# A two-layer perceiver on one core: small vector operations go to GpSimd, ScalarE and PSUM, and TensorE takes half the sums of the last recurrence

## The chip, the cores and the metric

The kernel runs on one core of one Trainium2 chip. Five engines of the core matter here. TensorE (PE in the profile; PEld is its weight load) multiplies matrices into PSUM, the accumulator memory of eight banks. VectorE (DVE) and ScalarE (ACT) read and write both SBUF and PSUM. GpSimd (POOL) works on SBUF here. SyncE (SP) issues most DMAs. Each engine takes its instructions in one fixed order, and an instruction that waits holds all that stand behind it on its engine.

The metric is the device time of one execution in microseconds (us), as the median of several runs. Lower is better.

## The reference, cut to what matters

The input `x` is 64 sequences of 32 tokens of 256 channels, that is 2048 tokens; `ctx` is 64 context sequences of 257 rows. Six layers follow each other, each added to `x`:

```python
x = x + cross_attention(layernorm(x), ctx, mask)        # stage 0 of the kernel
x = x + rwkv(layernorm(x))                              # stage 1
x = x + top2_experts(layernorm(x))                      # stage 2
x = x + quantized_cross_attention(layernorm(x), ctx)    # stage 3
x = x + state_space(layernorm(x))                       # stage 4
x = x + top1_experts(layernorm(x))                      # stage 5
```

Three details are touched by the change. Every layernorm (and the RMS norm inside the quantized attention) needs `1/sqrt(v + eps)`. The quantized attention rounds its rows to integers before a projection:

```python
scale = 127.0 / max(max(abs(x)), 1e-05)                 # per row
x_int = clip(round(x * scale), -128.0, 127.0)
```

The state-space layer keeps, for each of 512 channels, 16 states, and sums them with `C`:

```python
h = exp(A[None] * dt[:, :, None]) * h + dt * B_t * x_t
y = einsum('bdn,bn->bd', h, C_t) + D * x_t              # n = 16 states
```

The last layer computes all 8 experts (256 to 512 to 256 channels) with an exact gelu between.

## The kernel before, in words

The 2048 tokens are 4 blocks (`NBLK`) of 512 tokens (`BT`). Within a block, token-major tiles have 128 tokens (`P`) on the partitions. Stages 0, 1 and 2 work on blocks; stage 3 on 8 halves of 256 tokens, each of two tiles of 4 sequences, cut into 32 steps that `run` (L757) takes in order; stages 4 and 5 on blocks again. `layers` (L1280) writes the order by hand: the steps of stage 3 are laid between the blocks of stages 2 and 4 (`on(8, True)` and the like), and the recurrence of one block (`recur`) stands beside the attention or the experts of another. The program is then laid out as one fixed list per engine by a scheduler, which goes by the order of the text and its own costs; engines meet at semaphores.

**`_rsqrt`** (L76) makes `1/sqrt` without a table: `v = scale * in + eps` (L85), a first guess from the integer bits of `v` by a shift (L87) and a multiply-add (L88), all on VectorE, and then three Newton steps of four operations (L90 to L93) on the engine `eng`, which is GpSimd unless the caller gives VectorE. `_stats` (L107) calls it for each layernorm; stage 3 calls it for `dq` and `dy`.

**Stage 3.** `queries` (L712) prepares a half: mean and variance, `x - mean` into `xn` (L722), the rounding in `_quant_rows` (L341), and the step size `dq` (L728, L729). `_quant_rows` takes the row maximum, its scale and reciprocal, multiplies each tile by it and adds a constant that rounds (L350), and takes the constant off again into bfloat16 (L351). `finish` (L767) does the same for the attention's output `y`, which the trace calls `o` (L781 to L785). `attend` (L801) prepares one tile: `kl` (L828) is a PSUM result times a row of step sizes, `klm` (L830) spreads it with a mask. `back` (L923) divides by the softmax sums: `rs` is multiplied by a weight scale (L931), then by `pl` (L932), spread, and brought to `rt` through TensorE and a ScalarE copy (L946).

**Stage 4.** `recur` (L1078) loops over 16 states `n` and, in each, over two pairs of 128-channel groups (`c2` = 0 and 2). For one pair GpSimd multiplies `g` = dt x times B (L1096, 128x1024); ScalarE writes `h` = exp(A dt) into PSUM (L1100), twice; VectorE scans it (L1101) and multiplies by C into `hc` (L1102), twice; GpSimd adds `hc` to `y` (L1107; the trace calls `y` `xc`). After the loop GpSimd multiplies by the gate `zs` (L1110), and TensorE projects (L1122, or `end`, L1141, for the last block). `h` has two PSUM buffers (`psh`). For blocks 0 to 2 `_norm` (L1118) then makes the normalized residual `xe`.

**Stage 5.** `block` (L1236) loops over 8 experts times 4 groups of 128 hidden channels: two matrix products into `u` (L1251), an evacuation with bias by ScalarE (L1253), one gelu for each expert's 4 groups (L1255), and two products into `acc` with the expert before (L1259). `u` lies in the pool `psu` (one bank) or `ps` (two banks, tag `s`): for blocks 2 and 3 two of three go to `ps`. At the end of a block the result is transposed back through `rT` (L1272) and written out (L1273, L1275). The text puts the last recurrence (`recur(3)`) between the experts of block 1 and block 2; the scheduler lays the experts of block 2 beside it, and the experts of block 3 come last.

Of the kernel before, what the change touches and what calls it, by code (L numbers as in the profile page):

```python
# [75 lines left out]
def _rsqrt(k, out, parts, tag, pool=None, eng=None):  # L76


    nc, pool, f = k.nc, pool or k.small, out.shape[-1]
    eng = eng or nc.gpsimd  # L80
    n = out.shape[0]
    v, r, t = (pool.tile([P, f], F32, name=f"rs_{q}", tag=f"rs_{q}{tag}")[:n] for q in "vrt")
    at = 0
    for in_, scale, eps in parts:
        nc.vector.tensor_scalar(v[:, at : at + in_.shape[-1]], in_, scale, eps, ALU.mult, ALU.add)  # L85
        at += in_.shape[-1]
    nc.vector.tensor_scalar(r.bitcast(I32), v.bitcast(I32), 1, None, ALU.logical_shift_right)  # L87
    nc.vector.tensor_scalar(r.bitcast(I32), r.bitcast(I32), -1.0, 1597463007.0, ALU.mult, ALU.add)  # L88
    for step in range(3):
        eng.tensor_tensor(t, r, r, ALU.mult)  # L90
        eng.tensor_tensor(t, t, v, ALU.mult)
        eng.tensor_scalar(t, t, -0.5, 1.5, ALU.mult, ALU.add)
        eng.tensor_tensor(out if step == 2 else r, r, t, ALU.mult)  # L93
# [247 lines left out]
def _quant_rows(k, src, floor, ints, am):  # L341


    nc, n = k.nc, src.shape[1]
    nc.vector.tensor_reduce(am, src, AX.X, ALU.max, apply_absolute_value=True)
    sc = k.small.tile([P, n], F32, name="qsc", tag=f"q_sc{n}")
    nc.vector.tensor_scalar(sc, am, floor, 1.0 / 127.0, ALU.max, ALU.mult)
    nc.vector.reciprocal(sc, sc)
    for t in range(n):
        nc.vector.tensor_scalar(src[:, t, :], src[:, t, :], sc[:, t : t + 1], MAGIC, ALU.mult, ALU.add)  # L350
    nc.vector.tensor_scalar(ints, src, MAGIC, 127.0, ALU.subtract, ALU.min)  # L351
# [318 lines left out]
def _stage3(k, w, tmp):  # L670
# [41 lines left out]
    def queries(h):  # L712
        b, j0 = divmod(2 * h, 4)
        v = halves[h] = Ctx()
        v.xs = [k.x[b][:, j, :] for j in range(j0, j0 + 2)]

        mv = _moments(k, v.xs, "3")
        xn = k.wk3.tile([P, 2, D], F32, name="xn3", tag="xn3")  # L720
        for f in range(2):
            nc.vector.tensor_scalar(xn[:, f, :], v.xs[f], mv[:, f, 0:1], None, ALU.subtract)  # L722
        v.xq = k.wk3.tile([P, 2, D], BF16, name="xq", tag="xq")
        am = k.small.tile([P, 2], F32, name="am", tag="q_am")
        _quant_rows(k, xn, 3.1622776e-11, v.xq, am)
        dq = v.dq = k.small.tile([P, 2], F32, name="dq", tag="dq")
        _rsqrt(k, dq, [(mv[:, :, 1], 1.0 + RMS_EPS, RMS_EPS * LN_EPS)], "3")
        nc.vector.tensor_tensor(dq, dq, am, ALU.mult)  # L728
        nc.vector.tensor_scalar(dq, dq, 1e-5, qsc, ALU.max, ALU.mult)  # L729
# [37 lines left out]
    def finish(xs, o4):  # L767
# [13 lines left out]
        _quant_rows(k, y, 1e-8, yq, am)  # L781
        dy = k.small.tile([P, 2], F32, name="dy", tag="dy")
        _rsqrt(k, dy, [(ss, 1.0 / D, RMS_EPS)], "3y")
        nc.vector.tensor_tensor(dy, dy, am, ALU.mult)
        nc.vector.tensor_scalar(dy, dy, 1e-5, osc, ALU.max, ALU.mult)  # L785
# [15 lines left out]
    def attend(g, j, xq, dq, o4):  # L801
# [25 lines left out]
        kl = k.small.tile([P, 4], F32, name="kl", tag="kl3")  # L827
        nc.vector.tensor_tensor(kl, last_ps[:, P : P + 4], kb[:, :, 2 * P], ALU.mult)  # L828
# [94 lines left out]
        def back():  # L923
# [7 lines left out]
            nc.vector.tensor_scalar(rs, rs, mw[:, 2:3], None, ALU.mult)  # L931
# [14 lines left out]
            nc.scalar.copy(rt.rearrange("p w g i l -> p w l g i"), rt_ps.rearrange("p w (l g i) -> p w l g i", l=2, g=2))  # L946
# [25 lines left out]
def _stage4(k, w, wk):  # L972
# [44 lines left out]
    def ahead(b):  # L1017
# [3 lines left out]
        v.mv, v.rstd = _stats(k, xs, "4")  # L1021
        x2 = [tmp([P, 2, D], "xn4") for _ in range(2)]
# [55 lines left out]
    def recur(b, v, mem=None):  # L1078
# [4 lines left out]
        own, more = (mem, 1) if mem else (wk, 0)  # L1083
        dtx = wk.tile([P, C, BT], F32, name="dtx", tag="dtx", bufs=1)
# [6 lines left out]
        for n in range(N):  # L1091
            bc = own.tile([P, 2, BT], F32, name="bc", tag="bc", bufs=2 + more)
            nc.sync.dma_start(bc, bc_rows[n].partition_broadcast(P))
            for c2 in range(0, C, 2):
                g = own.tile([P, 2, BT], F32, name="g", tag="g", bufs=2 + more)
                nc.gpsimd.tensor_tensor(g, dtx[:, c2 : c2 + 2], bc[:, 0:1, :].to_broadcast([P, 2, BT]), ALU.mult)  # L1096
                hc = own.tile([P, 2, BT], F32, name="hc", tag="hc", bufs=2 + more)
                for c in range(2):
                    h = ph([P, BT], "h")
                    nc.scalar.activation(h, dt, AF.Exp, scale=A[:, c2 + c, n : n + 1])  # L1100
                    nc.vector.tensor_tensor_scan(h, h, g[:, c, :], 0.0, ALU.mult, ALU.add)  # L1101
                    nc.vector.tensor_tensor(hc[:, c, :], h, bc[:, 1, :], ALU.mult)  # L1102
                if n == 0:
# [4 lines left out]

        for c2 in range(0, C, 2):
            nc.gpsimd.tensor_tensor(y[:, c2 : c2 + 2], y[:, c2 : c2 + 2], v.zs[:, c2 : c2 + 2], ALU.mult)  # L1110
# [6 lines left out]
        for j in range(4):  # L1117
            _norm(k, xn[j], xs[j], v.mv, v.rstd, j)  # L1118
# [43 lines left out]
def _stage5(k, w, out):  # L1162
# [12 lines left out]
    def ps(shape, name, free=False):  # L1175

        return k.ps.tile(shape, F32, name=name, tag="s") if free else k.psu.tile(shape, F32, name=name, tag="u")
# [58 lines left out]
    def block(b, v):  # L1236
# [3 lines left out]
        for n in range(E * H + H):  # L1240
            e, q = divmod(n, H)
            if e < E:
# [6 lines left out]
                u = ps([P, BT], "up", b >= 2 and n % 3 > 0)  # L1249
# [3 lines left out]
                nc.scalar.activation(hid[e][:, q, :], u, AF.Identity, bias=b1)  # L1253
                if q == H - 1:
                    nc.scalar.activation(hid[e], hid[e], AF.Gelu)  # L1255
# [10 lines left out]
        for j2 in range(0, 4, 2):  # L1266
            rT = ps([P, 2, D], "rT", b >= 1)
# [178 lines left out]
```

## Time and profile before

| | us |
|---|---|
| time, median of 3 runs | 2037.06 (2034.74 to 2038.57) |
| the profiled execution's own time | 2031.43 |
| its span, first to last instruction | 2029.6 |
| busy: PE / DVE / POOL / ACT | 1604.5 / 1372.5 / 1062.8 / 986.5 |
| GpSimd waiting for VectorE's first guess (L90 on L88) | 178.6, 41 times |
| first recurrence, beside attention and experts of stage 2 | 767 to 1015 |
| second recurrence, beside attention and experts of stage 5 | 1115 to 1345 |
| third recurrence, the same | 1420 to 1690 |
| last recurrence, beside the experts of block 2 | about 1716 to 1887 |
| the experts of block 3, alone | 1910 to the end |

How to read it. A stretch such as 767 to 1015 is in us from the first instruction. A row of the stretch view gives, for one stretch, its length and then the busy time of PE, PEld, DVE, ACT and POOL, each with its number of instructions in brackets, the granted TensorE clock as a share of full speed, the DMA share and GB/s. A row of a group gives line, engine, operation, output<-inputs, shapes and count, and behind the bar the busy time in us, the mean ns of one, and the engine's idle time just before it with what ended it. A row of one line's view gives the shortest, median and longest duration in ns.

### The profile page before, as it was taken

To read this page: it belongs to the slowest core of one execution; us is meant where nothing else is said; L and a number is where in the kernel's file an instruction comes from. 1 tells how busy PE (TensorE), PEld (TensorE's weight loads), DVE (VectorE), ACT (ScalarE), POOL (GpSimd) and SP (SyncE) were. 2 spreads that over 40 slices of the span, in tenths; PEclk is the share of its full clock that TensorE was granted. 3 is DMA by queue.
4 is the path that set the end of the run, shared out by engine and by line. 5 is a ranking of instruction groups with operands and counts; after the bars stand their busy time and mean duration, and the time that the engine had idled before them with its cause. 6 is when DMAs were issued, how large, how long until landed. Compare 5 with 4: busy or idle time off the path is not lost. (4 is left out here: it accounts for less than half of the span.)

```text
span 2029.6 us, 20217 instructions
## 1 busy us (share of the span) xinstructions
PE 1604.5 (79%) x6323; PEld 820.7 (40%) x6323; DVE 1372.5 (68%) x2475; ACT 986.5 (49%) x2144; POOL 1062.8 (52%) x1189
## 2 busy tenths in 40 slices
PE   4775957759989888766788878878879777788698
PEld 3333524425645543433344434443434324333443
DVE  4588587576475458989965877864777786687400
ACT  3454443313455254444427746736647545576232
POOL 5344656413133215776650776871576766899200
PEclk9677877868989988556689778989779888899799
DMA  6764324210000201121101212401122212333021
GB/s 226 231 187 145 115 73 146 64 42 22 21 21 1 63 28 42 53 63 52 53 26 54 73 53 83 114 21 48 63 50 77 82 53 54 104 118 104 31 83 42
DMA packets 88379, 151.26 MB, mean 75 GB/s; under 512 B 7740, under 2 KB 52300, under 8 KB 86224
## 3 DMA queue, kind: packets, MB, share of 16 engines
q1 hardware_dynamic: 85428, 148.75, 24.0%
q10 hardware_dynamic: 2844, 1.22, 0.2%
q8 instruction: 50, 0.82, 0.2%
q14 instruction: 57, 0.47, 0.1%
HBM read 139.03 MB, written 10.92 MB: 74 GB/s over the span
## 5 line engine op out<-in xcount | busy, mean ns | idle before, releaser
L1096 POOL TENSOR_TENSOR g<-dtx,bc 128x1024 f32<-128x1024 f32 x128 | 301.3, 2357 | 156.4 <-DVE h L1101 82.1
L1101 DVE TENSOR_TENSOR_SCAN h<-h,g 128x512 f32<-128x512 f32 x256 | 306.8, 1218 | 59.7 <-ACT h L1100 57.3
L1107 POOL TENSOR_TENSOR xc<-xc,hc 128x1024 f32<-128x1024 f32 x128 | 302.5, 2364 | 32.4 <-DVE hc L1102 23.8
L1251 PE MATMUL up<-xT,w 128*128 128x512 f32 x512 | 276.9, 660 | 16.7 <-ACT hid L1253 16.6
L1259 PE MATMUL acc<-hid,w 128*128 128x512 f32 x512 | 268.6, 649 | 25.4 <-ACT hid L1255 25.4
L1100 ACT ACTIVATE h<-dt,A 128x512 f32<-128x512 f32 x256 | 172.5, 692 | 146.9 <-DVE hc L1102 146.5
L892 ACT ACTIVATE p<-sc,nm 128x256 f32<-128x256 f32 x256 | 118.0, 473 | 134.4 <-DVE nm L888 120.5
L881 PE MATMUL sc<-kT,qm 32*128 32x256 f32 x512 | 145.0, 491 | 34.9 <-DVE od L921 24.7
L1102 DVE TENSOR_TENSOR hc<-h,bc 128x512 f32<-128x512 f32 x256 | 169.1, 678 | 1.6
L1259 PEld LDWEIGHTS acc<-hid,w 128*128 128x128 f32 x512 | 100.6, 207 | 146.0 <-issue 103.0
L631 PE MATMUL weps<-we,xT 128*128 128x512 f32 x256 | 147.7, 703 | 14.1 <-DVE x L627 7.7
L1251 PEld LDWEIGHTS up<-xT,w 128*128 128x128 f32 x512 | 99.8, 208 | 129.2 <-issue 97.7
L90 POOL TENSOR_TENSOR rs_t<-rs_r 128x4 f32<-128x4 f32 (+4 forms) x168 | 37.6, 227 | 190.0 <-DVE rs_r L88 178.6
L1253 ACT ACTIVATE hid<-up,chan 128x512 f32<-128x512 f32 x128 | 86.4, 682 | 103.3 <-PE up L1251 103.2
L881 PEld LDWEIGHTS sc<-kT,qm 32*128 32x128 f32 x512 | 85.2, 228 | 86.0 <-DVE od L921 36.5
L907 PE MATMUL pt_ps<-ident,p 128*128 128x128 f32 x512 | 93.9, 316 | 26.2 <-ACT p L892 18.8
L886 DVE TENSOR_REDUCE nm<-sc 128x2 f32<-128x512 f32 x128 | 86.2, 684 | 36.3 <-PE sc L881 35.6
L909 ACT COPY pt<-pt_ps 128x512 f32<-128x512 f32 x128 | 74.3, 586 | 56.4 <-PE pt_ps L907 55.8
L907 PEld LDWEIGHTS pt_ps<-ident,p 128*128 128x128 f32 x512 | 65.2, 158 | 80.9 <-ACT p L892 39.1
L915 PE MATMUL oT_ps<-pt,v 128*32 128x128 f32 x1024 | 74.6, 313 | 19.0 <-ACT pt L909 18.9
L531 POOL TENSOR_TENSOR kk<-kk 128x512 f32<-128x512 f32 x32 | 34.2, 1074 | 105.7 <-ACT kk L530 102.8
L248 POOL TENSOR_TENSOR cT<-cT,scb 128x2056 f32<-128x2056 f32 x16 | 73.4, 4590 | 24.6 <-PE sc L259 15.6
(404 smaller groups left out, 3125.3 us busy)
## 6 DMA issues: line engine op xcount, KB each, us to landing
bc<-rows SPq DMA_DIRECT2D x64, 512.0 KB
w<-in_L_ffn_w_dram SPq DMA_DIRECT2D x64, 512.0 KB
cT<-in_ctxT_dram SPq DMA_DIRECT2D x16, 1028.0 KB
cq<-cq SPq DMA_DIRECT2D x32, 514.0 KB
cn<-in_ctx_dram SPq DMA_DIRECT2D x64, 256.0 KB
scb<-scales SPq DMA_DIRECT2D x16, 514.0 KB
kb<-steps SPq DMA_DIRECT2D x16, 514.0 KB
x<-in_x_dram SPq DMA_DIRECT2D x4, 512.0 KB
```

The lines of the kernel that those rows point to most:

```text
L631: nc.tensor.matmul(ps, xT[:, c, r], we[:, c, e : e + 2, :], start=c == 0, stop=c == 1)
L881: nc.tensor.matmul(sc[h][:, f, :], qm[r, e + f].rearrange("p l n g -> p (l n g)"), kTs[e][r, f, :], start=True, stop=True,)
L892: nc.scalar.activation(w_[:, f, h - h0, :], sc[h][:, f, :], AF.Exp, bias=nm[:, e + f, h : h + 1], accum_out=sm[:, e + f, h : h + 1],)
L907: nc.tensor.transpose(pt_ps[:, h, m, :], ws[e, hp][:, f, h, m * P : (m + 1) * P], k.ident)
L1096: nc.gpsimd.tensor_tensor(g, dtx[:, c2 : c2 + 2], bc[:, 0:1, :].to_broadcast([P, 2, BT]), ALU.mult)
L1100: nc.scalar.activation(h, dt, AF.Exp, scale=A[:, c2 + c, n : n + 1])
L1101: nc.vector.tensor_tensor_scan(h, h, g[:, c, :], 0.0, ALU.mult, ALU.add)
L1102: nc.vector.tensor_tensor(hc[:, c, :], h, bc[:, 1, :], ALU.mult)
L1107: nc.gpsimd.tensor_tensor(y[:, c2 : c2 + 2], y[:, c2 : c2 + 2], hc, ALU.add)
L1251: nc.tensor.matmul(u, w1[e][:, c, q * P : (q + 1) * P], xT[:, c, :], start=c == 0, stop=c == 1)
L1253: nc.scalar.activation(hid[e][:, q, :], u, AF.Identity, bias=b1)
L1259: nc.tensor.matmul(acc[o], w2[e][:, q, o * P : (o + 1) * P], hid[e][:, q, :], start=n == H, stop=n == E * H + H - 1)
```

## The change

1. `_rsqrt`: `v` and the first guess move from VectorE to `eng`; shift and multiply-add become one multiply-add by -0.5 on the integer bits.
2. `_quant_rows` takes an engine; for `y` in `finish` the rounding multiply-add goes to GpSimd.
3. In `queries`, `x - mean` becomes a ScalarE activation with a bias of minus the mean, which GpSimd makes; the two operations on `dq`, and the two on `dy`, go to GpSimd.
4. `kl` stays in the PSUM tile `last_ps`; the multiplication by the weight scale in `back` goes into the ScalarE copy that makes `rt`.
5. `xe` after a recurrence is made by ScalarE, from an offset that GpSimd makes in `ahead`.
6. In the last recurrence (`mem` is given), for the pair `c2` = 2, TensorE sums the `hc` of all states in two PSUM tiles `ys` of the pool `ps` by products with the identity, one state late; `D * x`, the sum and the gate are then done by four VectorE operations. `hc` gets a fourth buffer.
7. Since `ys` holds both banks of `ps`, the experts of block 2 use `psu` and `psp` (one bank each) in turn; block 3 uses four banks. In block 3 the gelu reads PSUM directly, one per group, with no separate pass.

```diff
@@ _rsqrt
-        nc.vector.tensor_scalar(v[:, at : at + in_.shape[-1]], in_, scale, eps, ALU.mult, ALU.add)
+        eng.tensor_scalar(v[:, at : at + in_.shape[-1]], in_, scale, eps, ALU.mult, ALU.add)
         at += in_.shape[-1]
-    nc.vector.tensor_scalar(r.bitcast(I32), v.bitcast(I32), 1, None, ALU.logical_shift_right)
-    nc.vector.tensor_scalar(r.bitcast(I32), r.bitcast(I32), -1.0, 1597463007.0, ALU.mult, ALU.add)
+    eng.tensor_scalar(r.bitcast(I32), v.bitcast(I32), -0.5, 1597463007.0, ALU.mult, ALU.add)
@@ _quant_rows(k, src, floor, ints, am, eng=None)
-        nc.vector.tensor_scalar(src[:, t, :], src[:, t, :], sc[:, t : t + 1], MAGIC, ALU.mult, ALU.add)
+        (eng or nc.vector).tensor_scalar(src[:, t, :], src[:, t, :], sc[:, t : t + 1], MAGIC, ALU.mult, ALU.add)
@@ _stage3, queries
+        minus = k.small.tile([P, 2], F32, name="minus", tag="minus3")
+        nc.gpsimd.tensor_scalar(minus, mv[:, :, 0], -1.0, None, ALU.mult)
         for f in range(2):
-            nc.vector.tensor_scalar(xn[:, f, :], v.xs[f], mv[:, f, 0:1], None, ALU.subtract)
+            nc.scalar.activation(xn[:, f, :], v.xs[f], AF.Identity, bias=minus[:, f : f + 1])
...
-        nc.vector.tensor_tensor(dq, dq, am, ALU.mult)
-        nc.vector.tensor_scalar(dq, dq, 1e-5, qsc, ALU.max, ALU.mult)
+        nc.gpsimd.tensor_tensor(dq, dq, am, ALU.mult)
+        nc.gpsimd.tensor_scalar(dq, dq, 1e-5, qsc, ALU.max, ALU.mult)
@@ finish
-        _quant_rows(k, y, 1e-8, yq, am)
+        _quant_rows(k, y, 1e-8, yq, am, nc.gpsimd)
...
-        nc.vector.tensor_tensor(dy, dy, am, ALU.mult)
-        nc.vector.tensor_scalar(dy, dy, 1e-5, osc, ALU.max, ALU.mult)
+        nc.gpsimd.tensor_tensor(dy, dy, am, ALU.mult)
+        nc.gpsimd.tensor_scalar(dy, dy, 1e-5, osc, ALU.max, ALU.mult)
@@ attend, back
-        kl = k.small.tile([P, 4], F32, name="kl", tag="kl3")
-        nc.vector.tensor_tensor(kl, last_ps[:, P : P + 4], kb[:, :, 2 * P], ALU.mult)
+        kl = last_ps[:, P : P + 4]
+        nc.vector.tensor_tensor(kl, kl, kb[:, :, 2 * P], ALU.mult)
...
-            nc.vector.tensor_scalar(rs, rs, mw[:, 2:3], None, ALU.mult)
...
-            nc.scalar.copy(rt.rearrange("p w g i l -> p w l g i"), rt_ps.rearrange("p w (l g i) -> p w l g i", l=2, g=2))
+            nc.scalar.activation(
+                rt.rearrange("p w g i l -> p w l g i"), rt_ps.rearrange("p w (l g i) -> p w l g i", l=2, g=2),
+                AF.Copy, scale=mw[:, 2:3],
+            )
@@ _stage4, ahead
+        v.off = k.small.tile([P, 4], F32, name="off", tag="off4")
+        nc.gpsimd.tensor_tensor(v.off, v.mv[:, :, 0], v.rstd, ALU.mult)
+        nc.gpsimd.tensor_scalar(v.off, v.off, -1.0, None, ALU.mult)
@@ recur
+        ys = [k.ps.tile([P, BT], F32, name="y_ps", tag="s") for _ in range(2)] if mem else None
+        late = []
+
+        def total(n, hc):
+            for c in range(2):
+                nc.tensor.matmul(ys[c], k.ident, hc[:, c, :], start=n == 0, stop=n == N - 1)
...
-                hc = own.tile([P, 2, BT], F32, name="hc", tag="hc", bufs=2 + more)
+                hc = own.tile([P, 2, BT], F32, name="hc", tag="hc", bufs=2 + 2 * more)
...
+                if mem and c2:
+                    late.append((n, hc))
+                    if len(late) > 1:
+                        total(*late.pop(0))
+                    continue
...
+        if mem:
+            total(*late.pop(0))
         for c2 in range(0, C, 2):
+            if mem and c2:
+                for c in range(2, C):
+                    nc.vector.scalar_tensor_tensor(y[:, c], y[:, c], _chan(k, "L1_attn_D", c), ys[c - 2], ALU.mult, ALU.add)
+                    nc.vector.tensor_tensor(y[:, c], y[:, c], v.zs[:, c], ALU.mult)
+                continue
             nc.gpsimd.tensor_tensor(y[:, c2 : c2 + 2], y[:, c2 : c2 + 2], v.zs[:, c2 : c2 + 2], ALU.mult)
...
-            _norm(k, xn[j], xs[j], v.mv, v.rstd, j)
+            nc.scalar.activation(xn[j], xs[j], AF.Identity, bias=v.off[:, j : j + 1], scale=v.rstd[:, j : j + 1])
@@ _stage5
-    def ps(shape, name, free=False):
+    def ps(shape, name, free=0):
 
-        return k.ps.tile(shape, F32, name=name, tag="s") if free else k.psu.tile(shape, F32, name=name, tag="u")
+        if free == 0:
+            return k.psu.tile(shape, F32, name=name, tag="u")
+        if free == 1:
+            return k.psp.tile(shape, F32, name=name, tag="p")
+        return k.ps.tile(shape, F32, name=name, tag="s")
...
-                u = ps([P, BT], "up", b >= 2 and n % 3 > 0)
+                u = ps([P, BT], "up", n % (1, 1, 2, 4)[b])
...
-                nc.scalar.activation(hid[e][:, q, :], u, AF.Identity, bias=b1)
-                if q == H - 1:
+                direct = b == NBLK - 1
+                nc.scalar.activation(hid[e][:, q, :], u, AF.Gelu if direct else AF.Identity, bias=b1)
+                if q == H - 1 and not direct:
                     nc.scalar.activation(hid[e], hid[e], AF.Gelu)
...
-            rT = ps([P, 2, D], "rT", b >= 1)
+            rT = ps([P, 2, D], "rT", (0, 2, 1, 2)[b])
```

More of the change, by code (lines that the diff above doesn't have):

```diff
@@ L338, in _stage0, with _quant_rows @@
     return block, steps
-def _quant_rows(k, src, floor, ints, am):
+def _quant_rows(k, src, floor, ints, am, eng=None):
     nc, n = k.nc, src.shape[1]
```

## The prediction, made blind

> **What bounds the kernel now.** I read the page's table of 40 slices first. No engine is full throughout, so the span was cut at the recurrences and the stretch view asked for each cut:
>
> ```profile
> 767.00:1015.00 248.00, 180.27 (x832) 97.76 (x830) 226.38 (x356) 116.93 (x307) 169.80 (x124) 0.66 0.19 54
> 1115.00:1345.00 230.00, 187.34 (x768) 90.31 (x767) 189.84 (x264) 141.50 (x306) 170.34 (x123) 0.81 0.25 74
> 1420.00:1690.00 270.00, 213.26 (x817) 100.88 (x818) 210.65 (x310) 158.38 (x305) 186.00 (x156) 0.86 0.22 63
> 1762.00:1887.00 125.00, 108.53 (x243) 47.41 (x241) 95.59 (x110) 83.97 (x104) 122.71 (x53) 0.95 0.36 109
> 1887.00:1910.00 23.00, 11.12 (x49) 9.75 (x50) 15.50 (x92) 1.17 (x2) 0.08 (x1) 0.71 0.07 23
> 1910.00:2030.00 120.00, 113.62 (x264) 49.59 (x263) 4.28 (x18) 39.84 (x44) 2.39 (x12) 0.97 0.18 57
> ```
>
> In the first recurrence VectorE (third pair of numbers) works 226.4 of 248 us: it is the bound. In the second and third it works 83% and 78%, beside a PE of about 80%. In the last one GpSimd works 122.7 of 125. The end is PE alone.
>
> Next, what VectorE's time in the first recurrence consists of, by groups, and two lines by their shortest, median and longest duration:
>
> ```profile
> L1102 DVE TENSOR_TENSOR hc<-h,bc 128x512 f32<-128x512 f32 x64 | 42.6, 676 | 0.0
> L87 DVE TENSOR_SCALAR rs_r<-rs_v 128x2 int32<-128x2 int32 x4 | 5.6, 1405 | 0.0
> L931 DVE TENSOR_SCALAR rp<-rp,mw 128x16 f32<-128x16 f32 x4 | 4.4, 1111 | 0.0
> ```
> ```profile
> L931 DVE TENSOR_SCALAR rp<-rp,mw x16: 217/234/2099, 517.7 to 1586.4; 128x16 f32<-128x16 f32 x16
> L1102 DVE TENSOR_TENSOR hc<-h,bc x256: 625/677/693, 773.1 to 1879.5; 128x512 f32<-128x512 f32 x128
> ```
>
> An operation on 2 or 16 elements takes over 1 us here although the same line's shortest is 0.22 us, and its longest, 2.10, is about one GpSimd operation of the recurrence (L1107, median 2.353). L1102, with one operand in PSUM, is never longer than 0.693 beside the same GpSimd operations. The timeline shows one case:
>
> ```profile
> 902.01 2.33 POOL L1107 TENSOR_TENSOR xc<-xc,hc 128x1024 f32<-128x1024 f32 x1
> 902.59 1.78 DVE L87 TENSOR_SCALAR rs_r<-rs_v 128x2 int32<-128x2 int32 x1
> 904.28 1.22 DVE L1101 TENSOR_TENSOR_SCAN h<-h,g 128x512 f32<-128x512 f32 x1
> ```
>
> L87 ends at 904.37, where GpSimd's operation does (904.34), and the scan behind it starts then. So a small SBUF-only VectorE operation can stand until GpSimd's current one is over, and the recurrence stands behind it.
>
> **Parts 1 to 5: VectorE's small operations.** What leaves VectorE, as busy us by groups in the three recurrences / in the whole span:
>
> - L85, L87, L88: 10.8, 9.3, 9.3 / 57.2. (58.5 in all; the four calls on VectorE keep two of three operations, 8 x 0.16 = 1.3.)
> - L722: 5.9, 1.1, 2.4 / 13.4. L931: 4.4, 2.5, 0.7 / 9.0. L350 on `o`: 4.3, 4.5, 3.3 / 16.2.
> - L728, L729, L784, L785: 1.1, 0.7, 3.1 / 9.9. L116 on `xe<-x`: 3.9, 2.5, 5.8 / 13.4.
> - L830 (`klm`) stays but reads `kl` from PSUM. By L1102 it should not be held; at its shortest, 0.157, it loses 5.0, 4.4, 3.8 / 13.7. That is the lower end of its cost; the upper is no gain.
>
> Sums: 35.4, 25.0, 28.4 / 132.8 us.
>
> Not all of a stall goes. L722, L931 and L350 are followed by other small SBUF operations (L347, L932, L351), which may be held instead. The time of the three above their shortest (0.34, 0.22, 0.32) is 11.7, 5.8, 3.7 us; I let two thirds of it move on: 7.8, 3.9, 2.5. What stays is 27.6, 21.1, 25.9. The guess operations are followed by scans and reductions from PSUM, so theirs goes entirely.
>
> A share reaches the end. In the first recurrence VectorE is idle only 9% of the time, so the share is near one; since every engine's order is laid out anew I take 0.6: **-16.5**. In the second and third VectorE idles 40 and 59 us, much of it for ScalarE's exponentials: 0.3 each, **-6.3** and **-7.8**. The remaining 44.0 us lie beside other bounds (PE busy 85% at 1015 to 1115 and at 1345 to 1420): 0.1, **-4.4**. The ends are none and all of 27.6 + 21.1 + 25.9 = 74.6.
>
> What is added. GpSimd gets two operations for each of 56 reciprocal roots at 0.2 us (L92's row) = 22 us, 16 roundings of `y`, and some 50 tiny operations, 10 us. A GpSimd multiply-add of this shape has a row, L502:
>
> ```profile
> L502 POOL TENSOR_SCALAR xn<-x,mv,r x16: 1217/1242/2287, 105.4 to 488.7; 128x256 f32<-128x256 f32 x16
> ```
>
> 16 x 1.24 = 20 us. GpSimd has 60 to 84 us idle in each of the first three recurrences, which hides this. Against L350's median of 0.344 on VectorE that is 3.6 times. The Trainium skill speaks against such a move: its page "GPSIMD Engine Reference", section "4.1 Engine selection", gives elementwise work to VectorE, though it calls GpSimd roughly line rate with one input. By line rate the roundings would cost an estimated 16 x 0.34 = 5.5 us in place of 20; the row decides, and either is hidden.
>
> ScalarE gets 28 activations of 128x256, 0.41 each (L779): 11.5 us, beside 40% and more idle. New waits: ScalarE's `xn` waits for GpSimd's `minus`, and behind it stand the exponentials of scores (L892) and recurrence (L1100), for which VectorE waits. `minus` may stand behind none to two GpSimd operations of 2.36; eight halves make 0 to 38 us. I take 0.5 us each, as queries are issued two steps before their use: **+4**. The scale in the copy to `rt` (0.19) is free.
>
> **Parts 6 and 7.** GpSimd loses 16 x 2.36 = 38 us in the last recurrence. But VectorE's own line there is 95.6 busy plus its waits:
>
> ```profile
> ACT h L1100 <- DVE hc L1102: 27.8, 18, 2.4
> DVE h L1101 <- ACT h L1100: 26.9, 27, 3.6
> ```
>
> 95.6 + 26.9 = 122.5 of 125: exponential, scan and product wait for each other through two PSUM buffers, and ScalarE's gelu with its two table loads (1.91 + 2 x 1.28) breaks them once an expert. GpSimd and this ring are equally long, so the 38 us buy almost nothing: the ring is late next. TensorE gets 16 x 2 products, 64 instructions at 0.43 (the steady spacing at the end) = 27.5 us, and has 16.5 us idle in this stretch and 11.9 in the next: 28.4. It fits if experts of block 2 slide into 1887 to 1910, which lies waiting for norm and router. Cost between 0 and 27.5; I take +1, since the list scheduler can put experts later. Two instead of three banks for `u`: with sums between, two groups of an expert take some 8 us, more than ScalarE's longest absence of 4.5, so nothing, or a part of the same 27.5.
>
> The tail: the last pair's add and gate on GpSimd end at 1887.1, VectorE's last `hc` at 1880.1. Through TensorE 1.7 and four VectorE operations of 0.7 it is 1884.6: -2.4. The roots on VectorE at 1890 to 1905 lose four operations: -0.7. The last expert's products wait 1.0 us for its gelu (L1259 on L1255): -1.0 with gelus straight from PSUM; no row shows such a gelu, but ScalarE is 67% idle there, so a slow one costs nothing. Together **-3**, ends -4 and +24.
>
> **The sum.** -16.5 - 6.3 - 7.8 - 4.4 + 4 - 3 = -34.0, against the profiled execution's 2031.43: 1997.4. The median shown is 5.6 above that execution: **2003 us**.
>
> **Rivals.**
> - *More of it counts*: all of 27.6 and 0.7 of 21.1 and 25.9 makes -60.5 - 4.4 + 4 - 3 = -64: 1973. For: VectorE at 91%. Against: its waits on ScalarE in the later ones.
> - *The stalls move on*: the next SBUF operation is held instead, and only the shortest durations are saved: 47 of 132.8 us, 35% of -35, so -12 + 4 - 3 = -11: 2026. For: L932 is held too (longest 2.16).
>   The Trainium skill, page "SBUF — State Buffer", section "SBUF: two separate sides", speaks for this rival: it calls the port pair of VectorE and GpSimd an exclusive lock for a whole instruction, so the next operation with two SBUF inputs would pay in the place of the one removed. The case at 902.59 above agrees with the lock; by it alone the sum would be this rival's.
> - *TensorE is short*: the 27.5 us find no room. +11 (over 16.5) to +24: 2014 to 2031.
> - *Off the path*: VectorE's relief is not where the end is set; about +1: 2038.
> - *GpSimd's queue becomes the gate* (slower): 16 new hops (`minus` to ScalarE, rounding to VectorE, one of each a half) stand behind one recurrence operation each, 16 x 2.36 = 38, and the roundings take 16 x (1.24 - 0.34) = 14 longer: 52 in place of 4. -38 + 52 = +14: 2051. It decides from (38 - 14 + 4) / 16, about 1.7 us a hop, on. For: GpSimd is 68 to 74% busy with 2.36 us operations. Against: it now waits 178.6 us for VectorE's first guesses, which no longer come from there.
>
> **Chances.** Forecast (1985 to 2020) 0.38; more counts 0.10; stalls move 0.14; TensorE short 0.08; off the path 0.12; queue gate 0.18. Off the path splits 0.02 faster, 0.07 same, 0.03 slower; 0.2% is 4 us, about what a measurement of this kernel can tell. Faster 0.38 + 0.10 + 0.14 + 0.08 + 0.02 = 0.72, same 0.07, slower 0.18 + 0.03 = 0.21. The range 1980 to 2045 leaves out most of the first rival (0.07) and two thirds of the gate (0.12): 0.19.
>
> **What would show it.** Right: the first recurrence's stretch some 17 us shorter, `klm` near 0.2 us, no VectorE first guess, GpSimd's waits for it gone, the last block's products without a gap. Wrong: L932, L351 or L347 at over 1 us (stalls moved); ScalarE idle before `xn` released by `minus`, and the score exponentials late behind it (gate); PE solid and VectorE waiting for a buffer of `hc` in the last recurrence (TensorE short); a last block that starts later than 1910 less the gains before it.

## The result, and the profile after

The changed kernel takes 2046.2 us (2035.5 to 2052.7) against 2037.7 of before in the same runs: ratio 1.003, 95% interval 1.0019 to 1.0041. It is slower by some 6 us in the mean, which the ratio goes by, and by 8.5 us in the median, where 34 less were forecast. Its profiled execution took 2044.4 us with a span of 2042.6, 13.0 us longer than that of before; that difference is larger because the profiled execution of before, 2031.4, was shorter than any of the 20 runs (2033.7 to 2043.7). Lines after L88 are shifted in the changed kernel; its recurrence is L1110 (`g`), L1114, L1115, L1116 (`hc`) and L1126 (the add), its `dtx` L1101.

The stretches of the prediction, cut at the same times in the changed kernel:

```profile
767.00:1015.00 248.00, 180.12 (x838) 98.12 (x836) 216.40 (x343) 128.45 (x320) 180.16 (x147) 0.70 0.19 57
1115.00:1345.00 230.00, 186.91 (x825) 91.35 (x826) 173.98 (x252) 154.31 (x330) 178.48 (x149) 0.87 0.27 78
1420.00:1690.00 270.00, 207.12 (x817) 100.58 (x818) 200.93 (x285) 159.99 (x311) 196.89 (x195) 0.83 0.21 59
1762.00:1887.00 125.00, 111.55 (x263) 48.12 (x262) 104.61 (x169) 69.39 (x87) 84.81 (x37) 0.99 0.31 85
1887.00:1910.00 23.00, 22.04 (x70) 10.86 (x69) 5.89 (x36) 11.53 (x14) 2.78 (x14) 1.00 0.28 86
1910.00:2043.00 133.00, 127.61 (x308) 56.25 (x306) 3.68 (x8) 28.27 (x40) 0.00 (x0) 0.99 0.21 67
```

VectorE is busy for 10, 16 and 10 us less in the first three rows, and GpSimd for 38 us less in the fourth: the relief is there. PE's 23 us stretch is now full (22.04, was 11.12), and the last row has 127.6 us of PE where it had 113.6.

Two VectorE operations by their shortest, median and longest duration in ns; in the kernel before, `klm` and then `sm`:

```profile
L830 DVE TENSOR_TENSOR klm<-kl,bmask x16: 157/708/2320, 478.6 to 1528.1; 128x16 f32<-128x16 f32 x16
```
```profile
L929 DVE TENSOR_TENSOR sm<-sm,rp x16: 156/176/1942, 517.2 to 1584.9; 128x16 f32<-128x16 f32 x16
```

and in the changed kernel:

```profile
L831 DVE TENSOR_TENSOR klm<-last_ps,bmask x16: 158/164/176, 490.8 to 1536.2; 128x16 f32<-128x16 f32 x16
```
```profile
L930 DVE TENSOR_TENSOR sm<-sm,rp x16: 143/622/2192, 530.7 to 1593.7; 128x16 f32<-128x16 f32 x16
```

`klm` from PSUM is no longer held, its median is 0.164 us as forecast. But `sm`, a sum of two SBUF operands a few operations on, which had a median of 0.176, now has 0.622: `klm` lost 13.5 us of its 16.2 in all, and `sm` gained 6.8, so half of this stall moved on. The Trainium skill, page "SBUF — State Buffer", section "SBUF: two separate sides", has one lock for a whole instruction on the port pair of the two engines; both pairs of rows agree with it.

GpSimd's longest waits between 700 and 1730 us (us in total, times, longest), in the kernel before:

```profile
POOL dtx L1087 <- DVE dt L1068: 84.3, 3, 40.8
POOL g L1096 <- DVE h L1101: 76.8, 26, 6.6
POOL rs_t L90 <- DVE rs_r L88: 66.7, 20, 20.7
```

and in the changed one:

```profile
POOL dtx L1101 <- DVE dt L1074: 105.0, 3, 45.0
POOL g L1110 <- DVE h L1115: 48.2, 20, 4.2
POOL rs_v L85 <- DVE mv L102: 31.5, 10, 7.0
POOL rs_v L85 <- DVE ms L1249: 26.0, 3, 13.1
```

The waits for the first guess (66.7) are gone from the list and stand there again one step earlier, as waits for the statistics `mv` and `ms` (57.5). And the first line grew from 84.3 to 105.0: GpSimd stands at the start of a recurrence, `dtx`, until `dt` is there. That line matters most for parts 1 to 5. One of these waits in GpSimd's timeline, changed kernel:

```profile
1095.72 0.20 POOL L92 TENSOR_TENSOR ms<-rs_r,rs_t 128x4 f32<-128x4 f32 x1
1116.18 3.32 POOL L1101 TENSOR_TENSOR dtx<-xc,dt 128x1024 f32<-128x1024 f32 x1 [20.26 <-DVE dt L1074]
1119.55 0.13 POOL L1103 MEMSET dt<- 128x16 f32 x1
1119.62 4.66 POOL L1110 TENSOR_TENSOR g<-dtx,bc 128x1024 f32<-128x1024 f32 x2
```

The second recurrence starts when `dt` comes, at 1116, and not when the first one is over, at 1008. From the single instructions of each trace (attention's end is the last `wo_ps` product of a block; a recurrence goes from its first to its last `hc`; us):

| block | 0 | 1 | 2 | 3 |
|---|---|---|---|---|
| before: attention ends | 705 | 1059 | 1362 | 1627 |
| recurrence | 773.1 to 1010.0 | 1126.2 to 1346.0 | 1436.1 to 1677.8 | 1724.8 to 1880.2 |
| changed: attention ends | 724 | 1062 | 1357 | 1637 |
| recurrence | 787.2 to 1008.2 | 1130.9 to 1340.7 | 1443.0 to 1664.1 | 1733.6 to 1869.8 |
| parts 1 to 5 alone: attention ends | 725 | 1059 | 1354 | 1633 |
| recurrence | 788.0 to 1005.2 | 1128.0 to 1336.7 | 1439.5 to 1660.3 | 1730.1 to 1870.6 |

The account of the 13 us, changed against before: recurrences -15.9, -10.1, -20.6 and -19.2, together -65.8; the three gaps between them +41.2; the start of the first +14.1; the time from the last `hc` to the end of the span +23.4 (149.4 to 172.8). Together +12.9. The recurrences shrank together by more than forecast, and each next one waited longer.

One entry needs care. Of the last recurrence's 19.2 us, 13.4 lie at its first state. In the kernel before, VectorE waits there for a root of the router (`ms`) and then does the router's operations:

```profile
1724.82 0.69 DVE L1102 TENSOR_TENSOR hc<-h,bc 128x512 f32<-128x512 f32 x1
1732.77 0.19 DVE L1221 TENSOR_TENSOR lg<-lg,ms 128x32 f32<-128x32 f32 x1 [7.27 <-POOL ms L93]
```

In the changed kernel the router is through before the first `hc`. So the second state, at 1745.7 before, 1741.1 in the changed kernel and 1737.6 without sums, is the fairer mark there: from it to the last `hc` the changed kernel's last recurrence is 5.8 us shorter.

### The profile page after: what moved, and what is told of

Its sections match the earlier page's. It is cut to its first block, busy times and chain, and to the rows that moved or that the text cites. A ratio compares the mean times of both kernels' runs of the same rounds, so it can differ in the third digit from the quotient of the medians.

```text
span 2042.6 us, 20282 instructions
## 1 busy us (share of the span) xinstructions
PE 1603.6 (79%) x6387; PEld 820.5 (40%) x6387; DVE 1279.5 (63%) x2211; ACT 979.9 (48%) x2157; POOL 1072.6 (53%) x1352
## 5 line engine op out<-in xcount | busy, mean ns | idle before, releaser
L1110 POOL TENSOR_TENSOR g<-dtx,bc 128x1024 f32<-128x1024 f32 x128 | 301.0, 2356 | 129.8 <-DVE h L1115 70.4
L1115 DVE TENSOR_TENSOR_SCAN h<-h,g 128x512 f32<-128x512 f32 x256 | 307.0, 1218 | 51.1 <-ACT h L1114 40.5
L1126 POOL TENSOR_TENSOR xc<-xc,hc 128x1024 f32<-128x1024 f32 x112 | 264.1, 2359 | 30.8 <-DVE hc L1116 26.3
L1290 PE MATMUL acc<-hid,w 128*128 128x512 f32 x512 | 259.8, 628 | 8.6 <-ACT hid L1286 8.4
L1114 ACT ACTIVATE h<-dt,A 128x512 f32<-128x512 f32 x256 | 173.6, 692 | 144.7 <-DVE hc L1116 142.4
L1116 DVE TENSOR_TENSOR hc<-h,bc 128x512 f32<-128x512 f32 x256 | 170.2, 680 | 4.0 <-POOL xc L1126 1.1
L893 ACT ACTIVATE p<-sc,nm 128x256 f32<-128x256 f32 x256 | 118.0, 473 | 113.6 <-DVE nm L889 104.8
L630 PE MATMUL weps<-we,xT 128*128 128x512 f32 x256 | 142.4, 681 | 18.1 <-DVE x L632 11.3
L882 PE MATMUL sc<-kT,qm 32*128 32x256 f32 x512 | 132.3, 454 | 21.9 <-DVE kT L861 10.5
L882 PEld LDWEIGHTS sc<-kT,qm 32*128 32x128 f32 x512 | 78.7, 211 | 74.2 <-issue 19.2
L1304 DVE SCALAR_TENSOR_TENSOR last<-rT,gt,x 128x256 f32<-128x256 f32 x16 | 7.4, 480 | 135.6 <-PE rT L1303 135.4
```

The costliest lines, as they stand in the source:

```text
L630: nc.tensor.matmul(ps, xT[:, c, r], we[:, c, e : e + 2, :], start=c == 0, stop=c == 1)
L882: nc.tensor.matmul(sc[h][:, f, :], qm[r, e + f].rearrange("p l n g -> p (l n g)"), kTs[e][r, f, :], start=True, stop=True,)
L893: nc.scalar.activation(w_[:, f, h - h0, :], sc[h][:, f, :], AF.Exp, bias=nm[:, e + f, h : h + 1], accum_out=sm[:, e + f, h : h + 1],)
L1290: nc.tensor.matmul(acc[o], w2[e][:, q, o * P : (o + 1) * P], hid[e][:, q, :], start=n == H, stop=n == E * H + H - 1)
```

## The experiments

Each has its median beside that of the kernel before on the same chip, and the ratio with its interval.

**What do the sums on TensorE cost?** Theory A: TensorE is short from the last recurrence on. Theory B: the loss lies ahead of it.

Parts 1 to 5 alone (parts 6 and 7 undone):

```diff
-        ys = [k.ps.tile([P, BT], F32, name="y_ps", tag="s") for _ in range(2)] if mem else None
+        ys = None
...
-                u = ps([P, BT], "up", n % (1, 1, 2, 4)[b])
+                u = ps([P, BT], "up", 2 if b >= 2 and n % 3 > 0 else 0)
-                direct = b == NBLK - 1
+                direct = False
```

> Parts 1 to 5 alone: the sums of the last recurrence, the banks and the gelus are as before the change. Two theories. (A) TensorE is short: in the changed kernel TensorE is busy without a gap from the last recurrence to the end, and the 64 products that sum (33.6 us busy) push the experts of block 2 behind the recurrence. Then this kernel is faster than the changed one by some 8 to 18 us: 2028 to 2038 us, and the last block's experts start once the router is through, with a gap before them. (B) The relief of VectorE is lost ahead of the last recurrence, since the order laid out anew gives it back between 1671 and 1726 us, and the last recurrence is neutral: 2043 to 2050 us, as the changed kernel. By the prediction's own terms (-35 + 4 of 2037) it would be 2006.

Measured: 2026.7 against 2037.1, 0.9948 (0.9931 to 0.9965).

Parts 6 and 7 alone (the kernel before, with the hunks of `recur`, `ps` and `block`):

> Parts 6 and 7 alone (sums on TensorE, other banks, gelus from PSUM); VectorE's small operations stay as before. (A) TensorE is short: the 33.6 us of products meet some 20 us of TensorE's idle time in 1726 to 1910 us, so slower than before by 8 to 16 us: 2045 to 2053 us. (B) Parts 6 and 7 are neutral: 2033 to 2040 us. By the prediction's term for them (-3): 2034.

Measured: 2045.4, 1.0041 (1.0024 to 1.0059).

The changed kernel with sums in bfloat16:

```diff
-                hc = own.tile([P, 2, BT], F32, name="hc", tag="hc", bufs=2 + 2 * more)
+                small = mem and c2
+                hc = own.tile([P, 2, BT], BF16 if small else F32, name="hc", tag="hcb" if small else "hc", bufs=2 if mem else 2)
...
-                nc.tensor.matmul(ys[c], k.ident, hc[:, c, :], start=n == 0, stop=n == N - 1)
+                nc.tensor.matmul(ys[c], k.identb, hc[:, c, :], start=n == 0, stop=n == N - 1)
```

> The changed kernel with its sums in bfloat16: hc of the second pair and the identity are rounded to bfloat16, so the sums are less exact; the number of products, their places and GpSimd's relief stay. (A) TensorE is short: each product takes less time (an estimate: half to a quarter of 0.43 us), so 17 to 25 us of the 33.6 come back, and the time falls to 2022 to 2033 us. (B) The loss lies ahead of the last recurrence: 2043 to 2049 us, as the changed kernel.

Measured: 2024.9, 0.9949 (0.9932 to 0.9967).

The changed kernel with half the states summed on TensorE:

```diff
-                nc.tensor.matmul(ys[c], k.ident, hc[:, c, :], start=n == 0, stop=n == N - 1)
+                nc.tensor.matmul(ys[c], k.ident, hc[:, c, :], start=n == 1, stop=n == N - 1)
...
-                if mem and c2:
+                if mem and c2 and n % 2:
                     late.append((n, hc))
...
-                    nc.vector.scalar_tensor_tensor(y[:, c], y[:, c], _chan(k, "L1_attn_D", c), ys[c - 2], ALU.mult, ALU.add)
+                    nc.vector.tensor_tensor(y[:, c], y[:, c], ys[c - 2], ALU.add)
```

> The changed kernel with only the odd states of the second pair summed on TensorE (32 products in place of 64); the even ones are added on GpSimd as before. (A) TensorE is short: the 16.8 us of products fit in the 20 us of idle time that TensorE had in 1726 to 1910 us without the sums, so the time is that of the run without sums or up to 5 us less: 2022 to 2030 us. If the price goes with the number of products from the first on: about half of +17, 2033 to 2038 us.

Measured: 2032.6 against 2038.6, 0.9974 (0.9957 to 0.999).

A holds for parts 6 and 7. Up to the last recurrence the changed kernel and the one without sums have the same order of instructions, so 2046 against 2027 is the price of parts 6 and 7 there: about 17 us by the two ratios; without parts 1 to 5 it is 8. In the traces the time behind the last `hc` grows alike, from 149.4 to 169.2 us and, with parts 1 to 5, from 152.5 to 172.8; what differs is how much shorter the last recurrence becomes, 10.3 and 4.4 us. With half the sums some 5 to 6 us of the price remain, between the two cases that were written down. With bfloat16 sums nothing is left of it, though the banks are those of the changed kernel; so the time of the products is the price, and not the two banks for `u`. (That kernel's order also differs in the earlier stages: its first recurrence starts at 782.7, and that of the kernel with half the sums at 782.5.) And 2027 without sums is 21 us above the 2006 of the prediction's own terms: most of the relief of parts 1 to 5 is lost as well. The sums in the changed kernel (with the first of VectorE's operations behind them), and then in bfloat16:

```profile
L1096 PE MATMUL y_ps<-hc,ident x64: 592/592/1061, 1762.7 to 1870.6; 128*128 128x512 f32 x64
L1133 DVE SCALAR_TENSOR_TENSOR xc<-xc,chan,y_ps x2: 740/743/746, 1870.4 to 1871.8; 128x512 f32<-128x512 f32 x2
```

```profile
L1096 PE MATMUL y_ps<-hc,identb x32: 376/377/379, 1752.7 to 1871.0; 128*128 128x512 bf16 x32
```

A float32 product is two instructions, which start 0.43 us apart back to back; a bfloat16 product is one, 0.215 us before the next. So the 32 products (the 64 of the expectations are instructions) hold TensorE for 27.5 us or for 6.9. The Trainium skill, page "FP8 and Floating Point Precision", section "TensorE Precision Notes", says that true float32 takes four passes; the ratio of 0.86 to 0.215 agrees.

Where the 27.5 us go is seen in TensorE's timeline at the end of the last recurrence (start, us, merged runs of one line; in brackets the idle time before). The changed kernel:

```profile
1874.70 3.62 PE L1173 MATMUL outps<-w_L_attn_out_projT,xc 128*128 128x256 f32 x16
1878.15 1.88 PE L1290 MATMUL acc<-hid,w 128*128 128x512 f32 x4
...
1919.78 7.03 PE L1290 MATMUL acc<-hid,w 128*128 128x512 f32 x16
1926.73 0.33 PE L1303 MATMUL rT<-ident,last 128*128 128x128 f32 x1
```

and the one without sums:

```profile
1883.43 7.89 PE L1290 MATMUL acc<-hid,w 128*128 128x512 f32 x18
1891.24 0.44 PE L1303 MATMUL rT<-ident,last 128*128 128x128 f32 x2
...
1894.73 0.67 PE L1231 MATMUL t_ps<-ident,xn 128*128 128x128 f32 x4
1897.26 0.69 PE L1231 MATMUL t_ps<-ident,xn 128*128 128x128 f32 x2 [1.86 <-DVE xn L115]
...
1902.38 13.78 PE L1281 MATMUL up<-xT,w 128*128 128x512 f32 x26
```

Without sums block 2's results are transposed (`rT`) at 1891, TensorE then waits for norm and router, and block 3 starts at 1902. With sums TensorE is still at block 2's experts at 1926. The stretches without sums:

```profile
1762.00:1887.00 125.00, 110.87 (x259) 50.88 (x260) 91.92 (x126) 82.33 (x99) 115.94 (x51) 0.96 0.39 101
1887.00:1910.00 23.00, 18.70 (x56) 10.15 (x55) 12.48 (x75) 5.44 (x8) 2.76 (x14) 0.78 0.18 56
1910.00:2023.00 113.00, 106.77 (x253) 46.83 (x251) 1.75 (x4) 38.33 (x41) 0.00 (x0) 0.99 0.19 61
```

From 1762 to its end TensorE has 236.3 us of work in 261, in the changed kernel 261.2 in 281: 24.9 us more work, 20 us later, of which 3.5 already lie between the starts of the two last recurrences. GpSimd's relief buys little: the last recurrence takes 136.1 us with sums and 140.5 without. The ring of exponential, scan and product is late next, as forecast: of the 125 us from 1762, VectorE is busy for 104.6 and waits for ScalarE for 15.7:

```profile
DVE h L1115 <- ACT h L1114: 15.7, 17, 2.8
```

**Block 3's gelus and four banks alone**, on the kernel before; below also on parts 1 to 5 with an old first guess, on parts 2 to 5, and on a merged guess:

```diff
-                u = ps([P, BT], "up", b >= 2 and n % 3 > 0)
+                u = ps([P, BT], "up", (2 if n % 3 > 0 else 0) if b == 2 else n % 4 if b == 3 else 0)
-                nc.scalar.activation(hid[e][:, q, :], u, AF.Identity, bias=b1)
-                if q == H - 1:
+                direct = b == NBLK - 1
+                nc.scalar.activation(hid[e][:, q, :], u, AF.Gelu if direct else AF.Identity, bias=b1)
+                if q == H - 1 and not direct:
```

> Only block 3's half of part 7: its gelus straight from PSUM and four banks for u; everything else as before the change. Both theories: TensorE's products of the last block run without a gap anyway, so -1 (the last gelu's wait) to 0: 2034 to 2039 us. If a gelu read from PSUM is slow or one per group holds u's banks, TensorE waits for hid and it is 2040 to 2050 us.

Measured: 2034.8, 0.9992 (0.9981 to 1.0003). On the other three, by their ratios, they moved the time by some -2, -3 and +4 us. A gain is not shown.

**Where did the gain of parts 1 to 5 go?** First the delay of 14 us ahead of the first recurrence. The roots of stages 0 and 1 get their old first guess back, on parts 1 to 5, without and with block 3's gelus:

```diff
+EARLY = ("0", "l", "s", "1", "1b")
...
+    if tag in EARLY:
+        nc.vector.tensor_scalar(r.bitcast(I32), v.bitcast(I32), 1, None, ALU.logical_shift_right)
+        nc.vector.tensor_scalar(r.bitcast(I32), r.bitcast(I32), -1.0, 1597463007.0, ALU.mult, ALU.add)
```

> Parts 1 to 5 as in the run without sums, but the reciprocal roots of stages 0 and 1 make v and the first guess on VectorE again, with three operations, as before the change. In the run without sums TensorE's events stand 13 to 15 us later than before from 400 to 780 us, and the first recurrence then makes up some 19. (C) The delay comes from these guesses: they stand in GpSimd's queue beside 4.6 us operations, and the order of stages 0 and 1 is laid anew by them. Then the delay goes and most of it reaches the end: 2011 to 2019 us. (D) The delay is made up again anyway, since the stretch up to the end of the first recurrence is set by something that the delay does not move: 2024 to 2030 us, as the run without sums.

> The first kernel of this group (parts 1 to 5, roots of stages 0 and 1 as before) with block 3's gelus straight from PSUM and its four banks, which alone gave -2 us. No sums on TensorE. (C) 2009 to 2018 us, the fastest so far. (D) 2022 to 2028 us.

Measured: 2026.4, 0.9937 (0.9923 to 0.995), and 2023.5, 0.9925 (0.9909 to 0.994), against 2039.0. The first recurrence does start 10 us earlier (777.5, 788.0), and the last one at the same time (1730.8, 1730.1): nothing of the 10 us arrives. The time is D's, but D's reason holds only in part: 6 of the 10 us are still there at the end of the first recurrence (999.1, 1005.2) and 5 at the start of the second (1123.0, 1128.0); at the end of the second they are gone (1337.4, 1336.7).

This run is also the cleanest test of parts 1 to 5, as its first recurrence reaches the second state when that of the kernel before does. From the second state on (us):

| | 0 | 1 | 2 | 3 |
|---|---|---|---|---|
| before: second state | 788.1 | 1136.9 | 1460.5 | 1745.7 |
| last `hc` | 1010.0 | 1346.0 | 1677.8 | 1880.2 |
| parts 1 to 5, early guess back: second state | 788.9 | 1137.4 | 1460.6 | 1738.3 |
| last `hc` | 999.1 | 1337.4 | 1661.2 | 1871.3 |

The first three recurrences are 11.7, 9.1 and 16.7 us shorter, together 37.5; the next ones begin 0.5 and 0.1 us later and 7.4 us earlier. So what is taken off a recurrence is given back in the gap behind it, but for those 7 us. What holds attention and the projections in that gap is not shown.

**Which of parts 1 to 5 counts?** Parts 2 to 5 (the three first lines of the guess undone), the same with block 3's gelus, and part 1 alone:

> Parts 2 to 5 alone: rounding of y, dq and dy on GpSimd, x minus mean and xe on ScalarE, klm from PSUM, the scale in the copy; reciprocal roots as before. (C) no delay in stages 0 and 1, and two thirds of what leaves VectorE in the recurrences: 2012 to 2024 us. (E) the roots' first guesses on VectorE were what GpSimd and the recurrence waited for, and without their move little is won: 2030 to 2038 us.

> Parts 2 to 5, and block 3's gelus from PSUM with four banks; roots as before, no sums on TensorE. -1.5 to -3 against the run of parts 2 to 5 alone, since these gave -1.6 and -3 in the two runs so far: 2019 to 2023 us.

> Part 1 alone and whole: v and merged first guess of every root on GpSimd; everything else as before. By the prediction's terms it takes 10.8, 9.3 and 9.3 us off VectorE in the recurrences: some -10, 2025 to 2030 us. (H) The hop into GpSimd's queue costs, as the run with the late guesses alone gave: 2050 to 2070 us. (F) that +24 was one order: 2028 to 2045 us.

Measured: 2024.3, 0.9926 (0.9909 to 0.9943); 2019.4, 0.9913 (0.9888 to 0.9938); and 2073.2 against 2042.7, 1.0151 (1.0127 to 1.0174). So part 1 alone costs 31 us where 10 less were forecast, and parts 2 to 5 give 15. Together they give 11 (the run without sums): the parts do not add up. Part 1 for stages 2 to 5 only:

> Part 1 alone, and only for the roots of stages 2 to 5: v and first guess on GpSimd; stages 0 and 1 and all else as before. By the groups these operations are a third of what leaves VectorE in the recurrences (10.8, 9.3 and 9.3 of 35.4, 25.0 and 28.4 us), and each frees the scan behind it. If shares count as in the run without sums: 10 us or so of gain, 2024 to 2031 us. If the holding of small operations only moves to the next one: 2035 to 2039 us.

Measured: 2063.2, 1.0118 (1.0102 to 1.0134), outside of both cases written down. Next, the first guess stays on VectorE, but as one multiply-add: in all stages, in stages 2 to 5, with parts 2 to 5, and with block 3's gelus:

```diff
-    nc.vector.tensor_scalar(r.bitcast(I32), v.bitcast(I32), 1, None, ALU.logical_shift_right)
-    nc.vector.tensor_scalar(r.bitcast(I32), r.bitcast(I32), -1.0, 1597463007.0, ALU.mult, ALU.add)
+    nc.vector.tensor_scalar(r.bitcast(I32), v.bitcast(I32), -0.5, 1597463007.0, ALU.mult, ALU.add)
```

> Before the change, with one edit: the first guess is one multiply-add by -0.5 on VectorE in place of shift and multiply-add, so nothing moves between engines and VectorE loses one small operation a root (the groups: 5.6 of 226 us busy in the first recurrence, some 20 in the span). By work alone: -2 to -6, 2031 to 2036 us. (F) The order laid anew by any edit moves the time by more than the work does: it then falls outside of 2028 to 2039 us, to either side, and the +24 of the run with the late guesses alone is of this kind. (G) That +24 was the hop to GpSimd's queue: this kernel is within 2028 to 2037 us.

> The merged first guess on VectorE for the roots of stages 2 to 5 alone; stages 0 and 1 as before. Its counterpart with v and guess on GpSimd gave +24. (H) Where the guess runs in stages 2 to 5 decides: 2016 to 2026 us. (I) The merged guess gained by what it did to stages 0 and 1: 2032 to 2040 us. (F) the order decides, with no tie to the work: 2045 us or more would show it.

> Parts 2 to 5 as in the run without the moved guesses (ratio 0.9926), and the first guess as one multiply-add on VectorE. By work: -1 to -5 against that run, 2018 to 2023 us (against 2037 of before). (F) outside of 2014 to 2028 us.

> The merged first guess on VectorE (ratio 0.9894) with block 3's gelus from PSUM and four banks, which changed the order only in the last block and gave -1.6, -3 and -5 us: 2013 to 2017 us, the fastest of all. If the gelus' gain was scatter: 2018 to 2021 us.

Measured: 2017.8 against 2038.6, 0.9894 (0.9879 to 0.9908), the lowest ratio of all; 2041.8 against 2042.7, 0.9998 (0.9985 to 1.0012); 2022.5, 0.9927 (0.9905 to 0.9949); 2018.2, 0.9916 (0.9899 to 0.9933). The merged guess gains 21 us in all stages (17 in the kernel that also has the gelus) and nothing in stages 2 to 5 alone; it was not run in stages 0 and 1 alone. On top of parts 2 to 5 it adds nothing either (0.9927, 0.9926), though stages 0 and 1 have it there.

Is that the price of the operation, or of the order that the scheduler lays for any edit? Two kernels change the order and no work to speak of (a memset given twice at the start; the root for `dy` written ahead of the rounding), one does the shift twice:

```diff
-    nc.gpsimd.memset(k.ones, 1.0)
+    nc.gpsimd.memset(k.ones, 1.0); nc.gpsimd.memset(k.ones, 1.0)
```

> Before the change, with one memset on GpSimd given twice at the very start; nothing else. The work is the same, but the lists of all engines are laid out differently from the first stage on. (F) The order alone moves the time by 5 us or more, to either side: outside of 2033 to 2043 us. (G) Orders of the same work are alike: 2034 to 2042 us.

> Before the change, with the root for dy written ahead of the rounding of y in finish; the same instructions, another order from stage 3 on. (F) outside of 2033 to 2043 us. (G) 2034 to 2042 us.

> Before the change, with the shift of every first guess on VectorE done twice (the second writes the same value again): one more small operation a root, where the merged guess had one less and gave -21. If that was the price of the operation and of the holds that it suffers: +10 to +25, 2048 to 2063 us. (F) If it was the order: anywhere from 2015 to 2055 us, with no tie to the sign of the work; 2040 us or less speaks for it plainly.

Measured, against 2036.6: 2039.0, 1.0014 (0.9999 to 1.003); 2039.7, 1.0018 (1.0005 to 1.003); 2036.4, 0.9995 (0.9979 to 1.0012). One more small VectorE operation a root costs nothing, which speaks against 21 us as the price of one. The two other orders differ from before by 3 to 4 us, so a new order alone was not shown to be worth 20 or 30 either. Inside, an order moves more: with the root first the second recurrence starts at 1110.9, 15 us earlier than before, and at the last one's second state (1745.9, 1745.7) all of it has been given back. No account in the expectations fits every run: (F), the order, came in for the merged guess and for the shift done twice, (G) for the two orders, and part 1 alone lies above (H).

What the trace shows of part 1 alone, in GpSimd's waits between 700 and 1730 us:

```profile
POOL dtx L1086 <- DVE dt L1067: 115.8, 3, 43.5
...
POOL rs_v L85 <- DVE mv L102: 31.8, 9, 9.6
```

The roots were not slower: from the last statistics to the last operation of a layernorm's root a mean of 5.2 us (16 roots between 700 and 1720 us), before 6.3 (17); of `dy`'s, from its first operation on, 5.5 and 8.3 (7 each). VectorE is busy for 1327.7 us in place of 1372.5. Yet attention's ends stand 26, 16, 30 and 56 us later than before (731, 1076, 1392, 1683), and the recurrences with them. So the hop into GpSimd's queue did not make the roots longer; what makes part 1 alone cost 31 us stays open.

## Why the prediction was wrong, step by step

**"A share reaches the end"** is the step that failed for parts 1 to 5. Its sizes were met or exceeded: the first recurrence was forecast 16.5 us shorter and is 15.9, the second and third 6.3 and 7.8 and are 10.1 and 20.6. But a share of 0.6 or 0.3 takes it that the next stage starts when the recurrence ends. It starts when attention of its block is through and `dt` has been made, and between the starts of two recurrences lie 353.1, 309.9 and 288.7 us before and 343.7, 312.1 and 290.6 after. The last one starts at 1733.6, 8.8 us later than before; by its second state it is 4.6 us ahead, and 8.1 without sums. For the delay of 14.1 us ahead of the first recurrence the sum had no term. Measured, parts 1 to 5 give 11 us in place of 31 (35 of gain, 4 of `minus`). VectorE being 91% busy told what limits the recurrence, not what starts the next one. The row that said so was among GpSimd's waits, `dtx` on `dt` with 84.3 us; the prediction went by the one for the first guess instead.

**The waits for the first guess** were taken as relief to come ("which no longer come from there"). They were waits for what stands ahead of the guess, and moved there.

**Part 1's share** had the wrong sign: +31 alone, cause open. The reason given against the queue gate, waits that go away, did not hold, since they moved; the gate itself is not shown either, as the roots took less time, and ScalarE waited for `minus` once, for 22.8 us, at 472 us and so ahead of the first recurrence.

**"16 x 1.24 = 20 us"** for the roundings of `y` on GpSimd was too much. The row it went by, L502, has two operands of one value a row, the rounding only one:

```profile
L349 POOL TENSOR_SCALAR o<-o,qsc x16: 478/482/488, 632.2 to 1630.0; 128x256 f32<-128x256 f32 x16
```

That is 16 x 0.48 = 7.7 us; the prediction's other estimate, 5.5, was nearer. The term was taken as hidden, so the sum does not change.

**"I take +1"** for the sums is the step that failed for parts 6 and 7. The price of 27.5 us was about right (24.9 us more work on TensorE than without sums), and the cost lies within the stated ends of -4 and +24. The room was wrong: 28.4 us of idle time were taken as free to the last us. Of the 16.5 inside the recurrence only 3.0 were filled (PE busy 108.5, now 111.6), of the 11.9 behind it 10.9, and the rest of the price fell on the end. Measured: 17 us for parts 6 and 7 with parts 1 to 5, 8 without.

**The rest.** The stall moving on came true in part (`sm`). The small terms (-2.4, -0.7, -1.0) cannot be told apart. Of the rivals, two came true together, off the path for most of parts 1 to 5 and TensorE short for 6 and 7. Off the path was priced with nothing for the sums, at 2038, TensorE short with all of the relief, at 2014 to 2031; measured, they are -11 and +17, and that is slower. By number "the stalls move on" (-12 + 4 for parts 1 to 5) is near the -11 too, but its mechanism is not: without sums VectorE is busy for 1273.9 us in place of 1372.5, 99 less, where that rival saves 47.

## What to carry to other kernels

Before a stage is relieved, look up what releases the stage behind it: if the next one waits for another chain, a shorter stage makes a longer gap (here 37.5 us shorter, 7.4 of them arrived). A wait of one engine for a small operation of another is worth nothing until it is known what that operation itself waited for. Work given to the engine that alone sets the last stretch can be paid there although it looked idle before: 8 and 17 of 27.5 us here.

## What was not expected of the hardware

What surprised was not one row but the sum of small edits in a program laid out as one list per engine: the same first guess costs +31 us on GpSimd and gives -21 as one operation on VectorE, while one more operation, or another order of the same work, moves 0 to 4 us. Why was not found.
